# Context products of distances 3 and 4 made during attention and kept in DRAM, with every block folded

## Chip, core and metric

The kernel runs on one core of one Trainium2 chip. The metric is device time in microseconds (us) of one execution; where several runs are given, their median. The engines are called by the profile's names: PE is TensorE (PEld is its weight loads), DVE is VectorE, ACT is ScalarE, POOL is GpSimd, SP is SyncE, whose queue issues every DMA of this kernel.

## What is computed

The reference is a decoder layer with three residual stages, each followed by a layer norm. Shapes: x and the context are 16 x 256 x 512 (batch, sequence, width).

```
x = layernorm(x + attention(x, w_q, w_k, w_v, w_o))      # 16 heads of 32, causal, quantised projections
x = layernorm(x + xattn(ctx, ctx, x, ssm_kernel, D))     # below
x = layernorm(x + ffn(x, gamma, W))                      # RMS norm, 8-bit rounding, one product

# xattn: x and the context are read as 256 "channels" (32 heads of 8) of length 512
kv  = einsum('bhil,bhjl->bijhl', ctx, ctx)               # products of every pair of a head's 8 channels
y   = causal convolution of kv with ssm_kernel[h]  +  kv * D[h]
out = einsum('bijhl,bhil->bjhl', y, x)
```

In the second stage k and v are the same tensor, so the 8 x 8 products of a head are symmetric in i and j. They are stored by distance d = j - i modulo 8: distances 0 to 3 have 8 products each, distance 4 has 4, which makes 36 products by 16 batches = 576 columns (`NPAIR`).

## The kernel before

**First stage, attention.** Work goes by batch. `step(b)` (lines 538 to 598) is written out by hand in four groups g = 0 to 3, one for each set of four attention heads. The order of calls in it is the order of the instructions on every engine: in this part PE, ACT, DVE, POOL and SP each run their queue in program order, and an instruction that waits holds everything behind it on its engine. A group has `scan` of batch b+1 (PE scores, then row maxima on DVE, L341 and L346) and `weigh` of batch b (PE scores again, exponential on ACT L386 into a tile `p`, then on POOL two selects L390 and the sum `both` L396). `values` of a group (PE L409, L416) reads `p` and comes just ahead of the next group's `weigh`. In the last batch (`last_step`) the order differs: two `weigh` run before the first `values`.

The input of a later batch goes through: `fetch_x(b+3)` (DMA L233), scales on DVE, scaling on POOL (L182, in group 2), rounding on ACT (L188), and in group 3 `turn_in(b+3)`, two DMA transposes on SP (L279) into the tile `xit`. The first reader of `xit` is `project_qk` for that batch, called in group 0 of the next step (four PE matmuls, L293). `turn_out` (L473) is a like pair of transposes for the attention output in group 2.

The tiles `p` and `low` come from the pool `hp` with three buffers each.

**Second and third stage.** One loop over the 32 heads h (lines 1091 to 1126), again in a hand-written order. Head h needs the tile `kv` (its 576 columns for four blocks of 128 positions), made from the context `c` by ACT (squares, L760) and POOL (`multiply(k)` for k = 1, 2, 3; L754; `multiply(2)` also makes distance 4). `block(h, lb)` for lb = 0 to 3 makes the convolution on PE (`products`, L785: 2(lb+1) matmuls, which the trace lists as 4, 8, 12 and 16) into a PSUM tile `y` with two buffers, and `with_queries` (DVE, L797 to L812) multiplies by x into the tiles `own` (pool `op`, four buffers) and `turn`. `add` (POOL, L960) adds `turn` into `own`; for blocks in `FOLDED` a second instruction (L962) folds four parts into two. `read` (PE, L820) transposes and sums the parts of `own`: two transposes for a folded block, four for block 0, which isn't folded. PE's order in one turn of the loop is: block 0, read of block 2 of head h-1, block 1, read of block 3 of h-1, block 2, the feed-forward product of h-2 (L907), read of block 0 of h, block 3, read of block 1 of h. After these come norm and feed-forward on DVE and ACT.

The loads of head h+2 (`c` L745 and L746, `w` L749), one DMA transpose and one store of a result are on SP in each turn.

Of the kernel before, what the change touches and what calls it, by code (L numbers as in the profile page):

```python
# [9 lines left out]
F32 = mybir.dt.float32  # L10
BF16 = mybir.dt.bfloat16
AF = mybir.ActivationFunctionType
ALU = mybir.AluOpType
AX = mybir.AxisListType

P = 128
# [16 lines left out]
def decoder_kernel(ctx: ExitStack, tc: tile.TileContext, x, ctx_t, w_q, w_k, w_v, w_o, ker, d_skip, gamma, w_f, out):  # L33
# [6 lines left out]
    w_inv = const.tile([P, 5], F32, name="w_inv")  # L40
    q_scale = const.tile([P, 1], F32, name="q_scale")
    taps = taps_pool.tile([XH, E + P], F32, name="taps")

    kept = ctx.enter_context(tc.tile_pool(name="kept", bufs=1))
    x1t = kept.tile([P, XH, NB, XD, B], F32, name="x1t")
# [169 lines left out]
    att = ExitStack()  # L215
    qk = att.enter_context(tc.tile_pool(name="qk", bufs=3, side="right"))
    vp = att.enter_context(tc.tile_pool(name="vp", bufs=3, side="right"))
    hp = att.enter_context(tc.tile_pool(name="hp", bufs=3, side="right"))
    bp = att.enter_context(tc.tile_pool(name="bp", bufs=2, side="right"))
    ps_s = att.enter_context(tc.tile_pool(name="ps_s", bufs=1, space=PSUM, side="right"))  # L220
    NT = S // P
# [138 lines left out]
    def lay_turned(m, b):  # L360
        t = terms[b % 2]
        tp = ps.tile([P, S], BF16, name="tpn", tag="misc")
        for i in range(NT):
            nc.tensor.transpose(tp[:, i * P : (i + 1) * P], t[:, i, :], ident_h)
        m.low = hp.tile([P, S], BF16, name="low")
        nc.scalar.copy(m.low, tp)
# [156 lines left out]
    def keep(m, b, ts=(0, 1)):  # L523
        nh = P // XD
        for t in ts:
# [5 lines left out]
                tp.rearrange("p c (h i) -> p c h i", i=XD),  # L531
            )

    def on(stage, b, *more):
        if 0 <= b < B:
            stage(batches[b], *more)

    def step(b):


        on(scan, b + 1, 0)
        on(lay_turned, b, b)
        on(fetch_x, b + 3, b + 3)
        on(fetch_again, b - 1, b - 1)
        on(values, b - 1, NB - 1)
        on(begin_batch, b + 2)
        scale = project_qk(batches[b + 2], 0, (0,), wait=True) if b + 2 < B else None
        on(spread, b + 2, b + 2)
        on(save_sums, b - 1)
        on(moments, b - 2)  # L550
        if scale:
            scale()
        on(weigh, b, 0)
        if b < 2:
            weight_round(3 + b, 0)
        if b == 0:
            weight_size(4, nc.scalar)
        on(project_qk, b + 2, 1)
        on(normalize, b - 2)
        on(divide_sums, b - 1)  # L560
        on(divide, b - 1, 0)

        on(scan, b + 1, 1)
        on(divide, b - 1, 1)
        on(out_scales, b - 1)
        on(values, b, 0)
        on(weigh, b, 1)
        if b == 0:
            weight_scale(4, weight_total(ps, 4))
        if b < 2:  # L570
            weight_round(3 + b, 1)
            weight_store(3 + b, 0)
        on(project_qk, b + 2, 2)
        on(out_scaled, b - 1)
        on(keep, b - 2, b - 2)

        on(scan, b + 1, 2)
        on(fetch_scales, b + 3, b + 3)
        on(out_rounded, b - 1)
        on(turn_out, b - 1)  # L580
        on(project_v, b + 2, 0)
        on(values, b, 1)
        on(values_scale, b + 3)
        on(fetch_scaled, b + 3, b + 3)
        on(weigh, b, 2)
        on(project_v, b + 2, 1)
        on(project_qk, b + 2, 0, (1,))
        if b < 2:
            weight_store(3 + b, 1)

        on(scan, b + 1, 3)
        on(project_qk, b + 2, 3)
        on(lay, b + 1, b + 1)
        on(fetch_rounded, b + 3)
        on(turn_in, b + 3, b + 3)
        on(values, b, 2)
        on(weigh, b, 3)
        on(close, b - 1)

    def last_step():  # L600


        k, n, m = batches[B - 3 :]
        lay_turned(m, B - 1)
        moments(k)
        weigh(m, 0)
        fetch_again(n, B - 2)
        values(n, NB - 1)
        save_sums(n)
        weigh(m, 1)  # L610
        normalize(k)
        divide_sums(n)
        divide(n, 0)
        divide(n, 1)
        out_scales(n)
        weigh(m, 2)
        values(m, 0)
        out_scaled(n)
        weigh(m, 3)
        n.oi = [rounded(ap, "oq0", n.ots[0])]  # L620
        values(m, 1)
        n.oi.append(rounded(ap, "oq1", n.ots[1]))
        values(m, 2)
        n.oit = kp.tile([P, NT, NB, P], BF16, name="oit")
        for t in range(NT):
            transposed(ps, n.oit[:, t], n.oi[t])
        close(n)
        fetch_again(m, B - 1)
        keep(k, B - 3, (0,))
        values(m, 3)  # L630
        save_sums(m)
# [97 lines left out]
    with ExitStack() as l2:  # L729
# [2 lines left out]
        ps_y = l2.enter_context(tc.tile_pool(name="ps_y", bufs=2, space=PSUM, side="right"))  # L732
        pb = l2.enter_context(tc.tile_pool(name="pb", bufs=1, side="right"))
        gam = pb.tile([P, E], F32, name="gam")
        op = l2.enter_context(tc.tile_pool(name="op", bufs=4, side="right"))


        turns = [pb.tile([P, 4, P], F32, name=f"turn{i}") for i in range(NB)]
# [2 lines left out]
        def prepare(h):  # L741


            c = lp.tile([P, NB, EXT, B], F32, name="c")
            nc.sync.dma_start(c[:, :, 0:XD, :], ctx_t[h])  # L745
            nc.sync.dma_start(c[:, :, XD:EXT, :], ctx_t[h][:, :, 0 : EXT - XD, :])  # L746

            w = lp.tile([P, E], F32, name="w")
            nc.sync.dma_start(w, bass.AP(taps.tensor, taps.offset + h * (E + P), [[1, P], [1, E]]))  # L749

            kv = cp.tile([P, NB, NPAIR], F32, name="kv")

            def part(at, n, i, d):
                nc.gpsimd.tensor_tensor(  # L754
                    kv[:, :, at : at + n * B].rearrange("p c (i b) -> p c i b", b=B),
                    c[:, :, i : i + n, :], c[:, :, i + d : i + d + n, :], ALU.mult,
                )

            def square():
                nc.scalar.activation(  # L760
                    kv[:, :, 0:P].rearrange("p c (i b) -> p c i b", b=B), c[:, :, 0:XD, :], AF.Square
                )

            def multiply(k):
                part(k * P, XD, 0, k)
                if k == 2:
                    part(4 * P, 4, 0, 4)

            q = cp.tile([P, NB, EXT, B], F32, name="q")

            def copy(c=slice(0, NB)):
                nc.scalar.copy(q[:, c, 0:XD, :], x1t[:, h, c])
                nc.scalar.copy(q[:, c, XD:EXT, :], x1t[:, h, c, 0 : EXT - XD, :])

            return w, kv, q, multiply, copy, square

        FOLDED = (1, 2, 3)
        Y0 = E - HALF

        def products(lb, w, kv):  # L780
# [161 lines left out]
        def multiply(m, k):  # L942
            m.inputs[3](k)

        def copy(m, *blocks):
            m.inputs[4](*blocks)

# [14 lines left out]
                nc.gpsimd.tensor_tensor(own[:, 0:2, :], own[:, 0:2, :], own[:, 2:4, :], ALU.add)  # L962

        def read(m, lb):
            if lb == 0:

                m.tok = ps_k.tile([P, NB, P], F32, name="tok")
            total(lb, m.parts.pop(lb), m.tok)
# [11 lines left out]
        def roots_of(cols):  # L980
            roots = Roots()
            roots.quarter = sm.tile([P, 3], F32, name="quarter")
            roots.root = sm.tile([P, 3], F32, name="root")
            roots.cols = cols
            return roots

        def last_heads(three):

            early, prev, last = heads[XH - 3 :]
            one, end = roots_of(slice(0, 1)), roots_of(slice(0, 1))  # L990
            read(last, 2)
            read_all(last, 3)
            second_moments(last, three)
            engine_roots(three)
            second_centred(last)
            newton(three)
            second_max(last)
            inverse_roots(three)
            second_norm(last, three)
            finish(early, three, XH - 3)  # L1000
            feed_product(prev)
            feed_forward(prev, one)
            last.fit = fp.tile([P, NB, P], BF16, name="fit")
            transposed(ps2, last.fit, last.fi)
            engine_roots(one)
            newton(one)
            inverse_roots(one)
            finish(prev, one, XH - 2)
            feed_product(last)
            feed_forward(last, end)  # L1010
            engine_roots(end)
            newton(end)
            inverse_roots(end)
            finish(last, end, XH - 1, shared=True)
# [4 lines left out]
        first_head = heads[0]  # L1019
        with tc.manual_schedule(engines=by_hand):  # L1020
            load(first_head, 0)
            load(heads[1], 1)
            nc.sync.dma_start(gam, gamma.partition_broadcast(P))
            multiply(first_head, 1)
# [6 lines left out]
            for t in range(NT):  # L1031
# [2 lines left out]
                m.ots[t] = scaled(ap, f"oq{t}", m.o[:, t, :], m.mul_o[t])  # L1034
                if t == 0:
                    moments(n)
            multiply(first_head, 3)
            square(first_head)
            m.oit = kp.tile([P, NT, NB, P], BF16, name="oit")
            transposed(ps, m.oit[:, 0], rounded(ap, "oq0", m.ots[0]))  # L1040
# [30 lines left out]
            for h in range(XH):  # L1071
# [2 lines left out]
                on(load, h + 2, h + 2)  # L1074
                on(add, h - 1, 3)
                on(block, h, 0)
                on(read, h - 1, 2)
                on(multiply, h + 1, 1)
                on(square, h + 1)

                on(block, h, 1)
                on(add, h, 0)
                on(read, h - 1, 3)
# [11 lines left out]
                if h > 0:  # L1095
                    inverse_roots(roots)
                on(add, h, 1)
                on(read, h, 0)
                on(multiply, h + 1, 3)
                on(second_norm, h - 1, roots)  # L1100
                on(turn, h - 1)
                on(finish, h - 3, roots, h - 3)
# [44 lines left out]
```

## Time and profile before

| what | value |
|---|---|
| median of 3 runs | 865.26 us (864.24 to 866.11) |
| the profiled execution | 861.76 us, its span 860.0 us |
| mean granted TensorE clock | 0.988 |
| attention, one `step` | 25.1 us; PE busy 24.72, POOL 12.54 |
| second part, one head | 12.40 us; PE busy 12.26, DVE 10.87, POOL 11.53 |
| kernel's DMA traffic | 64.51 MB, mean 75 GB/s |

The profile shows one execution. A group line has: source line, engine, operation, tiles written <- read, shape, count, then busy time and mean duration. The timeline has start and duration in us, and in square brackets how long the engine sat idle ahead of the instruction and who released it. A line of the chain of waits has a start, a duration, and what the chain was in at that time. For a DMA on SP the duration is what the queue spends on issuing it; the landing is told apart. Line numbers are those of the kernel before.

### The profile page before, as it was taken

To read this page: it belongs to the slowest core of one execution; us is meant where nothing else is said; L and a number is where in the kernel's file an instruction comes from. 1 tells how busy PE (TensorE), PEld (TensorE's weight loads), DVE (VectorE), ACT (ScalarE), POOL (GpSimd) and SP (SyncE) were. 2 spreads that over 40 slices of the span, in tenths; PEclk is the share of its full clock that TensorE was granted. 3 is DMA by queue.
4 is the path that set the end of the run, shared out by engine and by line. 5 is a ranking of instruction groups with operands and counts; after the bars stand their busy time and mean duration, and the time that the engine had idled before them with its cause. 6 is when DMAs were issued, how large, how long until landed. Compare 5 with 4: busy or idle time off the path is not lost.

```text
span 860.0 us, 20228 instructions
## 1 busy us (share of the span) xinstructions
PE 803.8 (93%) x7754; PEld 555.9 (65%) x7754; DVE 690.5 (80%) x1889; ACT 427.0 (50%) x707; POOL 583.4 (68%) x652
## 2 busy tenths in 40 slices
PE   4889999999999999998878999999999999999993
PEld 3556666666666666665646767776777677777762
DVE  6757887788888778876666888988898889888885
ACT  6555655556565555655644334433443444344434
POOL 5265544545454454544639999999999999999980
PEclk9999999999999999999979999999999999999997
DMA  9111222333122222211320233223323332333211
GB/s 319 45 33 53 66 69 69 75 76 76 26 63 68 71 75 76 51 39 35 88 65 19 69 99 95 71 81 99 88 67 91 99 84 68 95 98 74 75 38 55
DMA packets 102207, 64.51 MB, mean 75 GB/s; under 512 B 66464, under 2 KB 83104, under 8 KB 102112
## 3 DMA queue, kind: packets, MB, share of 16 engines
q1 hardware_dynamic: 102112, 63.23, 27.5%
q8 instruction: 61, 1.00, 0.5%
q14 instruction: 34, 0.28, 0.1%
HBM read 43.34 MB, written 8.47 MB: 60 GB/s over the span
## 4 chain that ended last, share of the span: by engine, by line
PE 77%; DVE 10%; ACT 6%; issue 4%; POOL 2%; DMA 0%; ACTq 0%; DVEq 0%; POOLq 0%
PE y L785 32%; PE s L341 6%; PE acc L293 6%; PE s L381 5%; ACT p L386 4%; PE tok L820 4%; PE pv L409 4%; PE s L334 4%; PE acc_o L482 3%; DVE nmax L346 3%; PE acc_f L907 3%; PE sums L416 2%; PE s L374 2%; PE acc_v L311 2%; PE tp L528 1%
## 5 line engine op out<-in xcount | busy, mean ns | idle before, releaser
L785 PE MATMUL y<-kv,w 128*128 128x288 f32 x1280 | 335.0, 409 | 4.4 <-DVE turn L812 2.0
L785 PEld LDWEIGHTS y<-kv,w 128*128 128x128 f32 x1280 | 234.0, 191 | 64.9 <-PE tok L820 10.5
L960 POOL TENSOR_TENSOR own<-own,turn 128x512 f32<-128x512 f32 x127 | 161.7, 1274 | 21.1 <-DVE turn L812 11.0
L390 POOL TENSOR_SCALAR_AFFINE_SELECT p<-p 128x512 f32<-128x512 f32 x128 | 81.3, 659 | 139.5 <-ACT p L386 129.1
L754 POOL TENSOR_TENSOR kv<-c 128x512 f32<-128x512 f32 (+1 forms) x128 | 144.4, 1140 | 2.9 <-PE sums L416 2.9
L346 DVE TENSOR_REDUCE nmax<-s 128x4 f32<-128x512 f32 (+1 forms) x128 | 116.5, 952 | 35.5 <-PE s L341 35.5
L386 ACT ACTIVATE p<-s 128x1536 f32<-128x1536 f32 x64 | 92.9, 1452 | 70.3 <-PE s L381 70.2
L845 ACT ACTIVATE root<-quarter 128x3 f32<-128x3 f32 (+2 forms) x34 | 7.0, 204 | 159.5 <-DVE quarter L840 159.5
L396 POOL TENSOR_TENSOR both<-p 128x512 f32<-128x512 f32 x64 | 82.3, 1286 | 5.3
L797 DVE SCALAR_TENSOR_TENSOR own<-y,q 128x128 f32<-128x128 f32 x128 | 36.7, 286 | 50.5 <-PE y L785 42.6
L962 POOL TENSOR_TENSOR own<-own 128x256 f32<-128x256 f32 x95 | 69.1, 727 | 7.5
L293 PE MATMUL acc<-xit,w 128*128 128x256 bf16 x504 | 68.9, 276 | 3.6 <-DVE w L158 3.4
L800 DVE TENSOR_TENSOR own<-y,q 128x384 f32<-128x384 f32 x128 | 70.1, 548 | 0.0
L803 DVE TENSOR_TENSOR turn<-y,q 128x384 f32<-128x384 f32 x128 | 70.1, 548 | 0.0
L820 PEld LDWEIGHTS tok<-ident,own 128*128 128x128 f32 x318 | 37.7, 141 | 38.5 <-POOL own L962 26.0
L293 PEld LDWEIGHTS <-w 128*128 128x128 bf16 x512 | 45.9, 99 | 24.1 <-issue 8.5
L820 PE MATMUL tok<-ident,own 128*128 128x128 f32 x318 | 58.7, 283 | 2.4 <-issue 1.2
L341 PE MATMUL s<-kt,qt 32*128 32x128 f32 (+1 forms) x1024 | 60.0, 348 | 0.0
L381 PE MATMUL s<-qt,kt 32*128 32x256 f32 (+1 forms) x1024 | 57.4, 335 | 0.0
L409 PE MATMUL pv<-p,va 128*32 128x256 f32 (+1 forms) x1024 | 54.9, 332 | 0.0
L421 ACT COPY ot<-pv 128x256 f32<-128x256 f32 x64 | 23.9, 373 | 50.8 <-PE pv L409 50.2
L334 PE MATMUL s<-mask,ident_h 128*128 128x256 bf16 x256 | 38.3, 271 | 11.0 <-ACT p L386 9.9
(148 smaller groups left out, 1359.8 us busy)
## 6 DMA issues: line engine op xcount, KB each, us to landing
xt<-in_x SPq DMA_DIRECT2D x16, 512.0 KB, 4.1
xr<-in_x SPq DMA_DIRECT2D x16, 512.0 KB, 4.6
c<-in_ctx_t SPq DMA_DIRECT2D x32, 256.0 KB, 3.3
w<-taps SPq DMA_DIRECT2D x32, 256.0 KB, 4.1
out_y<-res SPq DMA_DIRECT2D x31, 256.0 KB, 2.3
c<-in_ctx_t SPq DMA_DIRECT2D x32, 128.0 KB, 3.2
x1t<-in_w_q SPq DMA_DIRECT2D x1, 1024.0 KB, 6.6
x1t<-in_w_k SPq DMA_DIRECT2D x1, 1024.0 KB, 9.4
```

What stands on the lines that cost most here:

```text
L293: nc.tensor.matmul(acc[:, j, :], w[:, c, o * P : (o + 1) * P], m.xit[:, c].rearrange("p t k -> p (t k)"), start=(c == 0), stop=(c == NB - 1),)
L341: nc.tensor.matmul(s[:, r, lo:hi], m.qt[rows, g, q0 : q0 + P], m.kt[rows, g, 0:nk], start=False, stop=True, skip_group_check=True,)
L346: nc.vector.tensor_reduce(m.nmax[:, t, :, g], s[:, :, cols], AX.X, ALU.max, negate=True)
L381: nc.tensor.matmul(s[:, r, lo:hi], m.kt[rows, g, k0 : k0 + P], m.qt[rows, g, q0:S], start=False, stop=True, skip_group_check=True,)
L386: nc.scalar.activation(p, s[:, :, 0 : 3 * P], AF.Exp)
L390: nc.gpsimd.affine_select(out=own, in_=own, compare_op=ALU.is_ge, fill=0.0, base=0, pattern=[[0, 4], [1, P]], channel_multiplier=-1,)
L396: nc.gpsimd.tensor_tensor(both, p[:, :, P : 2 * P], p[:, :, 2 * P : 3 * P], ALU.add)
L409: nc.tensor.matmul(acc[rows, q0:S], m.va[:, j, 4 * g + r, :], p[:, r, src], start=(j == 0), stop=(j == 1), skip_group_check=True, tile_pos ...
L754: nc.gpsimd.tensor_tensor(kv[:, :, at : at + n * B].rearrange("p c (i b) -> p c i b", b=B), c[:, :, i : i + n, :], c[:, :, i + d : i + d + ...
L785: nc.tensor.matmul(y[:, Y0 + k * HALF : Y0 + (k + 1) * HALF], lhs, kv[:, mb, k * HALF : (k + 1) * HALF], start=(mb == 0), stop=(mb == lb),)
L820: nc.tensor.matmul(tok[:, lb, :], lhsT=own[:, d, :], rhs=ident, is_transpose=True, start=(d == last), stop=(d == 0))
L960: nc.gpsimd.tensor_tensor(own[:, 0:4, :], own[:, 0:4, :], turns[lb], ALU.add)
```

## The change

1. A tile `far_d` in DRAM holds, for each of the 32 heads, the products of distances 3 and 4 (192 columns for each of four blocks, 384 KB a head).
2. From batch 2 on, attention makes these products: `far_load` (two DMAs) brings a head's context, `far_multiply` (two POOL instructions, 128x512 and 128x256) makes them, `far_store` (one DMA) writes them and issues the next head's load. POOL's part comes right after `weigh` of groups 0 and 2, and of group 3 in odd batches: 2 or 3 heads in a step, 32 in steps 2 to 14. The store and the next load are issued in the group after, just behind `scan`, and thus on SP ahead of what follows in that group. The tiles `far_c` and `far_kv` have one buffer each.
3. `hp` goes from three buffers to two.
4. In the head loop `multiply(3)` and the distance-4 part of `multiply(2)` are gone; `fetch_far` (one DMA a head) reads them from `far_d` into `kv`.
5. Block 0 is folded too (one more POOL instruction a head), its `read` has two transposes instead of four, and moves from ahead of block 3 to the next turn, behind block 0 of the next head. `op` goes from four buffers to five.

```diff
+    FAR = P + P // 2
+    far_d = taps_pool.tile([XH, P, NB, FAR], F32, name="far_d")
...
-    hp = att.enter_context(tc.tile_pool(name="hp", bufs=3, side="right"))
+    hp = att.enter_context(tc.tile_pool(name="hp", bufs=2, side="right"))
+    farp = att.enter_context(tc.tile_pool(name="farp", bufs=1, side="right"))
...
+    def far_load(h):
+        far.c = farp.tile([P, NB, SPAN, B], F32, name="far_c")
+        nc.sync.dma_start(far.c[:, :, 0:XD, :], ctx_t[h])
+        nc.sync.dma_start(far.c[:, :, XD:SPAN, :], ctx_t[h][:, :, 0 : SPAN - XD, :])
+
+    def far_multiply():
+        far.kv = farp.tile([P, NB, FAR], F32, name="far_kv")
+        for at, n, d in ((0, XD, 3), (P, 4, 4)):
+            nc.gpsimd.tensor_tensor(
+                far.kv[:, :, at : at + n * B].rearrange("p c (i b) -> p c i b", b=B),
+                far.c[:, :, 0:n, :], far.c[:, :, d : d + n, :], ALU.mult,
+            )
+
+    def far_store(h):
+        nc.sync.dma_start(far_d[h], far.kv)
+        if h + 1 < XH:
+            far_load(h + 1)
...
+    def far_step(b, g):
+        if b == 2 and g == 0:
+            far_load(0)
+        elif b >= 2 and far.stored < far.done:
+            far_store(far.stored)
+            far.stored += 1
+
+    def far_work(b, g):
+        if b >= 2 and far.done < XH and (g in (0, 2) or (g == 3 and b % 2)):
+            far_multiply()
+            far.done += 1
...
         on(scan, b + 1, 2)
+        far_step(b, 2)
...
         on(weigh, b, 2)
+        far_work(b, 2)
...
         on(scan, b + 1, 3)
+        far_step(b, 3)
         on(project_qk, b + 2, 3)
         on(lay, b + 1, b + 1)
         on(fetch_rounded, b + 3)
         on(turn_in, b + 3, b + 3)
         on(values, b, 2)
         on(weigh, b, 3)
+        far_work(b, 3)
...
-        op = l2.enter_context(tc.tile_pool(name="op", bufs=4, side="right"))
+        op = l2.enter_context(tc.tile_pool(name="op", bufs=5, side="right"))
...
             def multiply(k):
                 part(k * P, XD, 0, k)
-                if k == 2:
-                    part(4 * P, 4, 0, 4)
+
+            def fetch_far():
+                nc.sync.dma_start(kv[:, :, 3 * P : NPAIR], far_d[h])
...
-        FOLDED = (1, 2, 3)
+        FOLDED = (0, 1, 2, 3)
...
+            read(last, 0)
             read(last, 2)
             read_all(last, 3)
...
                 on(block, h, 0)
+                on(read, h - 1, 0)
                 on(read, h - 1, 2)
                 on(multiply, h + 1, 1)
                 on(square, h + 1)
 
+                on(fetch_far, h + 1)
                 on(block, h, 1)
                 on(add, h, 0)
                 on(read, h - 1, 3)
...
                 on(add, h, 1)
-                on(read, h, 0)
-                on(multiply, h + 1, 3)
```

The first head's own `multiply(3)`, in the passage between the two parts, is replaced by a `fetch_far` at its start. In groups 0 and 1 `far_step` and `far_work` stand at the like places.

More of the change, by code (lines that the diff above doesn't have):

```diff
@@ L532, in keep @@
             )
+    SPAN = XD + 3
+    class Far:
+        pass
+    far = Far()
+    def far_load(h):
[13 more added lines that the diff above has]
+            far_load(h + 1)
+    far.done = far.stored = 0
+    def far_step(b, g):
[8 more added lines that the diff above has]
+            far.done += 1
     def on(stage, b, *more):
@@ L541, in step @@
         on(scan, b + 1, 0)
+        far_step(b, 0)
         on(lay_turned, b, b)
@@ L553, in step @@
         on(weigh, b, 0)
+        far_work(b, 0)
         if b < 2:
@@ L563, in step @@
         on(scan, b + 1, 1)
+        far_step(b, 1)
         on(divide, b - 1, 1)
@@ L567, in step @@
         on(weigh, b, 1)
+        far_work(b, 1)
         if b == 0:
@@ L604, in last_step @@
         lay_turned(m, B - 1)
+        far_step(B - 1, 0)
         moments(k)
@@ L773, in copy @@
                 nc.scalar.copy(q[:, c, XD:EXT, :], x1t[:, h, c, 0 : EXT - XD, :])
-            return w, kv, q, multiply, copy, square
-        FOLDED = (1, 2, 3)
+            return w, kv, q, multiply, copy, square, fetch_far
+        FOLDED = (0, 1, 2, 3)
         Y0 = E - HALF
@@ L943, in multiply, with fetch_far @@
             m.inputs[3](k)
+        def fetch_far(m):
+            m.inputs[6]()
         def copy(m, *blocks):
@@ L964, in read @@
         def read(m, lb):
-            if lb == 0:
+            if not hasattr(m, "tok"):
                 m.tok = ps_k.tile([P, NB, P], F32, name="tok")
@@ L1021, in decoder_kernel @@
             load(first_head, 0)
+            fetch_far(first_head)
             load(heads[1], 1)
@@ L1036, in decoder_kernel @@
                     moments(n)
-            multiply(first_head, 3)
             square(first_head)
```

## The prediction

> **What bounds the kernel now.** I read the page's engine shares and its 40 slices first, then engine busy time in two long windows, the chain of waits through a head, and the timeline of one attention step. The windows (length, then busy time with instruction counts of PE, PEld, DVE, ACT, POOL; then clock, DMA share, GB/s) give:
>
> ```profile
> PE   4889999999999999998878999999999999999993
> POOL 5265544545454454544639999999999999999980
> 100.00:400.00 300.00, 294.23 (x4456) 197.64 (x4455) 243.66 (x473) 171.93 (x237) 148.82 (x189) 1.00 0.25 61
> 486.00:842.00 356.00, 351.81 (x1554) 251.85 (x1553) 312.13 (x1094) 149.47 (x315) 327.68 (x313) 1.00 0.30 81
> ```
>
> The reader is to see that PE is full in both parts (98% and 99%), while POOL is half empty in attention and 92% busy in the head loop. What counts is whose wait ends last. Through one head the chain stays on PE:
>
> ```profile
> 614.03 0.44 PE tok L820 x4
> 614.47 3.88 PE y L785 x16
> 618.35 0.22 PE tok L820 x2
> 618.57 0.97 PE y L785 x4
> 619.54 0.42 PE tok L820 x2
> 619.96 0.13 issue
> 620.09 2.18 PE y L785 x8
> ```
>
> PE ends block 3 (x16) at 618.35, but block 1 of the next head (x8) starts only at 620.09. It needs the `y` buffer that block 3 used, and DVE frees that one at 619.93 (timeline, last instruction of `with_queries`). DVE is thus a close second bound:
>
> ```profile
> 609.98 0.29 DVE L797 SCALAR_TENSOR_TENSOR own<-y,q 128x128 f32<-128x128 f32 x1 [1.04 <-PE y L785]
> ...
> 618.46 0.29 DVE L797 SCALAR_TENSOR_TENSOR own<-y,q 128x128 f32<-128x128 f32 x1 [0.22 <-PE y L785]
> ...
> 560.69 0.29 DVE L797 SCALAR_TENSOR_TENSOR own<-y,q 128x128 f32<-128x128 f32 x1 [1.39 <-PE tok L820]
> ...
> 568.87 0.29 DVE L797 SCALAR_TENSOR_TENSOR own<-y,q 128x128 f32<-128x128 f32 x1
> ```
>
> From block 1's L797 to block 3's is 8.48 us when DVE waits for PE, and 8.18 in the one head where it started late and waited for nothing. Attention, one step:
>
> ```profile
> 207.66 2.50 SPq L279 DMA_TRANSPOSE xit<-xq_i  x2
> 210.27 0.52 SPq L233 DMA_DIRECT2D xt<-in_x  x1
> ...
> 208.02 1.27 POOL L396 TENSOR_TENSOR both<-p 128x512 f32<-128x512 f32 x1
> 212.90 1.23 POOL L390 TENSOR_SCALAR_AFFINE_SELECT p<-p 128x512 f32<-128x512 f32 x2 [3.61 <-ACT p L386]
> ...
> 215.90 0.61 PE L293 MATMUL acc<-xit,w 128*128 128x256 bf16 x4
> ```
>
> The two transposes of the next batch are issued at 207.66, land by 211.4 (2.5 us after the second) and are read by PE at 215.90: 4.5 us to spare. POOL has a gap of 3.6 us between 209.29 and 212.90.
>
> **The change, part by part.** *Head loop, PE.* `read` of block 0 goes from four transposes to two; the 0.44 us between L907 and the 16 matmuls goes, and two transposes (0.22) come where PE now waits for DVE. So block 3 ends 0.44 earlier. What is late next is DVE: its 8.18 us from block 1 to block 3, then 3.92 (568.87 to 572.79) until block 1 of the next head. The loop becomes 8.18 + 3.92 = 12.10 instead of 12.40, a gain of 0.30 a head; not 0.44, since DVE takes the rest. PE alone would need less: 2.18 + 0.38 + 2.91 + 0.86 + 3.88 to the end of block 3, then 0.22 + 0.97 + 0.44 to block 1, 11.84. About 28 heads run in this steady state: 8.4 us. *Head loop, POOL.* Out go 1.28 (L754, 128x512) and 0.73 (128x256), in comes 0.73 (L962): 11.53 becomes 10.3, and POOL is never last. Only the first heads gain: at 449.1 to 453.3 the chain runs over POOL (L754 1.24, L960 1.25, then "issue" 1.18) to the `read` ahead of block 3, and PE is free from 452.1 while that block starts at 453.94. Of 1.8 I take 1.2, and 0.7 for the next two heads. Sum for the loop: -10.3, from -6 (0.2 a head, the idle time in brackets) to -14 (0.44 a head).
>
> *Head loop, DMA.* `fetch_far` (384 KB) is issued behind `w` at about 609.4. `w`, issued at 608.72, lands 4.4 us later, so the new one lands near 614.5; block 0 of the next head reads it at 618.4. Hidden; should that cover go, it costs what it is late in each head. In SP's order the DMA transpose L902 comes 8 us later, so nothing waits for it. The fifth `own` buffer covers the later `read`.
>
> *Attention, POOL.* 32 times 1.96 us (the L754 pair at 612.17) comes into 13 steps. The gaps behind `both` are 3.61 (group 2), 3.52 (group 0) and 2.21 (group 3), so each is covered: 0. In odd batches group 3's context lands at about 216 instead of 215.49, which eats its 0.25 of slack; at worst 0.5 in six steps, 3 us.
>
> *Attention, SP: the added wait.* In group 3 the store of group 2's products is ahead of `turn_in`. It waits for POOL, and behind it on SP stand the two loads, both transposes, then `xt` and `xr`. Step by step: `both` of group 2 ends at 209.29, the products at 211.25, SP sees it within 0.1 at 211.33. Issuing a store takes 0.62 to the next (as L927 to L745), the loads 0.62 and 0.74 (L745, L746), so the first transpose starts at 213.31 instead of 207.66, the second 1.25 later, landing 2.45 after that: 217.0. PE wants it at 215.90. The 4.5 us of slack become a stall of 1.1 us, and PE has nothing else in its order. It comes back every step because `both` moves with PE; it concerns steps 2 to 12 (`turn_in` ends with batch 15), 11 stalls. The transposes also share the queue with 736 KB just issued; `xt` and `xr`, 1024 KB, took 5.0 us from issue to landing, so some overlap is left. Ends: 0.5 (if each of the three DMAs took only the 0.41 of `xr`) and 2.5 (if the loads land at their slowest, 4.6 us, and the transposes' data all come behind). I take 1.4, near the unloaded sum: 11 x 1.4 = +15.4, from +5.5 to +27.5.
>
> The trace has `c` landing 3.2 us after issue (4.6 at most), here at 215.8, ahead of the transposes. [...]
>
> The other transposes (L473, 202.49) come behind a store that waits for group 0's products (198.7 in this step's time) and end their queue at 200.8: no loss. `xt` is late by 5 to 10 us, against a use 18 us after its issue: no loss.
>
> *Last step, two `p` buffers.* In steady state a group's `values` is ahead of the next `weigh`, so two suffice: 0. In `last_step` the exponential of group 2 (420.62) now waits for `values` of group 0 (421.2, +0.6), and that of group 3 (423.32) for `values` of group 1 (about 424.9, +1.6). Behind it on ACT is the rounding L188 (424.67), which is on the chain: +1.6, from 0 to +2.2.
>
> Sum: -10.3 + 15.4 + 1.6 = +6.7 against the profiled 861.76 us (span 860.0 and 1.8 around it), which lies 3.5 under the median of the runs shown. Put on the median: 865.26 + 6.7 = **872.0**.
>
> **Rivals.** (1) *Faster: SP is held for less.* The place is the store ahead of `turn_in`; the gain of 8.7 that is left without stalls is lost at 0.79 us a stall. For it: that is only 0.3 under my unloaded sum, and issue times of 0.41 exist. Against: three DMAs plus the 4.0 us POOL delay are all rows of this trace. With 0.3 a stall: 860; with none: 856.6. (2) *The loop keeps its time*: DVE's 8.18 was seen in one head only; if a head gains 0.1, the loop gives -5 and the time is 877 to 878. (3) *Transfers collide*: 2.5 us a stall gives 884. For it: 736 KB right ahead in the one queue; against: the data should be through at about 215.2. (4) *It doesn't do what it says*: the instruction order shows 64 more POOL multiplies in attention and 128 more DMAs, so no.
>
> **How the numbers follow.** Measurement can tell about 0.2%, 1.7 us. Forecast (stall of 1.0 to 2.0, 867 to 879): 0.60. Within 0.2% (stall near 0.8): 0.08. Rival 1: 0.17. Rival 2: 0.09. Rival 3: 0.06. Slower 0.60 + 0.09 + 0.06 = 0.75. Range 861 to 884: it takes in part of rival 1 and nearly all above.
>
> **What would show it.** In the profile after: L279's successor issued about 4.0 us after `both` of group 2 ends, PE's xit matmul with idle time put down to a DMA, the attention step at 26.5 instead of 25.1 for 11 steps; a head at 12.10 with no idle time ahead of block 3's L797; ACT's exponential waiting for PE in the last step. A step still at 25.1 proves the stall wrong; a head at 12.40 proves the DVE reading wrong; 11.84 would mean that PE alone sets it.

## The result and the profile after

The changed kernel takes 877.31 us (median of 4 runs, 875.94 to 880.7) against 865.08 us (median of 4, 864.24 to 866.11) of the kernel before in the same job: ratio 1.0147, 95% interval 1.0115 to 1.0178. It is slower. The profiled execution took 875.94 us with a span of 874.2, 14.2 more than the 860.0 of before.

The page's slices of PE and POOL for the changed kernel, and its busy time in a window of attention and one of the head loop (columns as before; line numbers from here on are those of the kernel that ran):

```profile
PE   4889999999888999999778999999999999999994
POOL 5265657666575675766663988898888888888880
100.00:400.00 300.00, 275.84 (x4100) 186.44 (x4136) 237.38 (x444) 162.22 (x225) 191.95 (x233) 0.99 0.50 127
500.00:850.00 350.00, 341.00 (x1476) 250.66 (x1503) 311.37 (x1098) 149.57 (x315) 298.29 (x290) 1.00 0.44 117
```

The reader is to see eights among the nines of PE in the first half: in attention PE fell from 98% to 92% busy, while POOL rose from 50% to 64%. In the loop PE goes from 99% to 97% and POOL from 92% to 85%. So the loss is in attention and isn't POOL's load. The marks below are DVE instructions, one in each attention step (the row maximum of the divided output) and one in each block (L849); times in us.

| stretch | before | after | difference |
|---|---|---|---|
| 11 attention steps | 276.0 | 297.6 | +21.6 |
| last full step to the first block of the loop | 26.1 | 29.8 | +3.7 |
| head loop, first block to last | 395.9 | 385.6 | -10.3 |

In the loop (timeline of DVE's L849 in one head; block 1 at 606.03, block 3 at 614.21, block 1 of the next head at 618.13) nothing is waited for ahead of block 3, and the head takes 12.10:

```profile
606.03 0.29 DVE L849 SCALAR_TENSOR_TENSOR own<-y,q 128x128 f32<-128x128 f32 x1 [1.05 <-PE y L837]
...
614.21 0.29 DVE L849 SCALAR_TENSOR_TENSOR own<-y,q 128x128 f32<-128x128 f32 x1
...
618.13 0.29 DVE L849 SCALAR_TENSOR_TENSOR own<-y,q 128x128 f32<-128x128 f32 x1 [1.04 <-PE y L837]
```

Attention now has a wait that before had none of. The waits view (waiting <- awaited: us in all, how often, longest) and the timeline of one of the milder steps:

```profile
PE acc L296 <- DMA xit<-xq_i: 13.5, 8, 2.7
ACT p L389 <- PE sums L419: 3.1, 2, 2.0
```

```profile
327.64 1.97 POOL L552 TENSOR_TENSOR far_kv<-far_c 128x512 f32<-128x512 f32 x2
...
329.63 0.37 SPq L558 DMA_DIRECT2D far_d<-far_kv  x1
...
330.11 0.57 SPq L546 DMA_DIRECT2D far_c<-in_ctx_t  x1
...
331.48 2.56 SPq L282 DMA_TRANSPOSE xit<-xq_i  x2
...
335.39 0.60 PE L296 MATMUL acc<-xit,w 128*128 128x256 bf16 x4 [1.00 <-DMA xit<-xq_i]
```

SP waits for POOL's products until 329.61, spends 1.85 us on the store and two loads, and only then starts the transposes, 3.80 us after `both` ended at 327.68; PE waits 1.00 for them. But the steps aren't alike. They took 26.72, 26.57, 26.52, **29.26, 27.38, 27.54, 28.89**, 26.11, 26.19, 26.26 and 26.19 us, against 25.09. The first of the four in bold:

```profile
192.28 2.58 SPq L282 DMA_TRANSPOSE xit<-xq_i  x2
...
197.92 1.01 PE L296 MATMUL acc<-xit,w 128*128 128x256 bf16 x4 [2.71 <-DMA xit<-xq_i]
...
199.37 1.59 PE L384 MATMUL s<-qt,kt 32*128 32x256 f32 x13
```

Here PE starts 5.64 us after the issue, not 3.91, and the same four matmuls take 1.01 us instead of 0.60: the granted clock is 0.5 from 197.9 to 201.3. So two things are to be explained that the forecast did not have: why the transposes land late in four steps, and what the slow clock costs.

### The profile page after: what moved, and what is told of

It is laid out like the page before. It is cut to its first block, busy times and chain, and to the rows that moved or that the text cites. A ratio compares the mean times of both kernels' runs of the same rounds, so it can differ in the third digit from the quotient of the medians.

```text
span 874.2 us, 20247 instructions
## 1 busy us (share of the span) xinstructions
PE 792.6 (91%) x7614; PEld 555.6 (64%) x7690; DVE 697.2 (80%) x1889; ACT 426.9 (49%) x707; POOL 605.9 (69%) x684
## 4 chain that ended last, share of the span: by engine, by line
PE 67%; DVE 10%; ACT 10%; issue 5%; POOL 4%; DMA 3%; ACTq 0%; POOLq 0%; DVEq 0%
PE y L837 29%; PE acc L296 6%; PE s L344 6%; PE s L384 5%; ACT p L389 4%; DVE nmax L349 4%; PE s L337 3%; PE acc_o L485 3%; DMA xit<-xq_i 3%; PE acc_f L959 3%; PE pv L412 3%; ACT res L978 2%; PE s L377 2%; ACT q L824 2%; PE acc_v L314 2%
## 5 line engine op out<-in xcount | busy, mean ns | idle before, releaser
L1017 POOL TENSOR_TENSOR own<-own 128x256 f32<-128x256 f32 x127 | 92.2, 726 | 9.9
L805 POOL TENSOR_TENSOR kv<-c 128x512 f32<-128x512 f32 x64 | 81.4, 1272 | 4.7 <-PE sums L419 4.7
L849 DVE SCALAR_TENSOR_TENSOR own<-y,q 128x128 f32<-128x128 f32 x128 | 36.7, 286 | 42.3 <-PE y L837 33.7
L552 POOL TENSOR_TENSOR far_kv<-far_c 128x512 f32<-128x512 f32 x64 | 62.8, 1002 | 6.6 <-DMA far_c<-in_ctx_t 6.2
L302 DVE SCALAR_TENSOR_TENSOR qt<-acc,q_scale,inv_row 128x256 f32<-128x256 f32 (+1 forms) x45 | 26.2, 582 | 31.2 <-PE acc L296 18.5
```

Of the source, the lines that this page charges most:

```text
L805: nc.gpsimd.tensor_tensor(kv[:, :, at : at + n * B].rearrange("p c (i b) -> p c i b", b=B), c[:, :, i : i + n, :], c[:, :, i + d : i + d + ...
```

## The experiments

Theory at the start: the far store and loads ahead of `turn_in` in group 3 cost the steps, by SP's wait and by their issue; the loop's gain is as forecast; the two `p` buffers cost the last step. Later a further point came in: a 16 KB packet of the instruction queue delays transposes that are in flight. Each ratio is against runs of the kernel before in the same job.

**1. The store and loads behind the transposes.**

```diff
         on(scan, b + 1, 3)
-        far_step(b, 3)
...
         on(turn_in, b + 3, b + 3)
+        far_step(b, 3)
         on(values, b, 2)
```

> The changed kernel with one call moved: in group 3 the store of the far products stands behind turn_in on SP instead of ahead of it. Same work, same traffic. Theory (the queue is held): the transposes of xit start again right after the rounding, some 4 us earlier, PE's wait for xit goes from every step and the attention step is 25.1 us again; 21.6 us of attention time and the half-clock windows that follow such waits go, so 877.3 - 21.6 = 855.7, 853 to 858. Rival (GpSimd's added work or the added traffic slows attention wherever the store stands): the step stays above 25.7 and the time above 863.

Measured: 855.62 us (854.71 to 858.1), ratio 0.9907, 0.9883 to 0.9931. Ten of the eleven steps take 25.13 or 25.14, and one 26.25, in which PE waited for DVE's row maxima. The order on SP, from the timeline:

```profile
209.06 2.50 SPq L282 DMA_TRANSPOSE xit<-xq_i  x2
...
210.62 1.97 POOL L552 TENSOR_TENSOR far_kv<-far_c 128x512 f32<-128x512 f32 x2
...
212.62 0.36 SPq L558 DMA_DIRECT2D far_d<-far_kv  x1
```

The transposes are out before the products are begun, and PE waits for them nowhere. All of the work and all of the transfers are still there, so in ten of the eleven steps neither POOL's 64 multiplies nor the traffic costs attention more than 0.04 us (and experiment 5 has the same 25.13 with the two `p` buffers alone): the place of one call costs it. What held DVE up in the one step stays open. Moved, the change is faster than before.

**2. Only the loads behind.** The store with its wait stays ahead of `turn_in`, the two loads go behind it.

```diff
-            far_store(far.stored)
+            far_store(far.stored, g != 3)      # False: without the next load
...
         on(turn_in, b + 3, b + 3)
+        far_late()                             # the load
         on(values, b, 2)
```

> The changed kernel with the store still ahead of turn_in in group 3, but the two loads behind it. Theory (the wait is the sum of POOL's products and the issue times): the loads' 0.62 + 0.74 us leave the path, the unloaded stall of 1.0 to 1.3 us becomes 0 to 0.2, and only steps in which the transposes land late (by 1 to 1.7 us) still stall; attention gives back 14 to 21 of its 21.6 us: 856 to 864, middle 860. Rival (a transpose behind a waiting store is late whatever stands between): the stall stays above 0.8 in every step and the time above 870.

Measured: 872.5 us (870.14 to 876.45), ratio 1.0113, 1.0074 to 1.0153. The reason held and the time did not. In five of the eleven steps the transposes now land 0.4 to 0.5 us before PE reads them: the wait and the store's issue, without the 1.3 us of load issues, just fit into the old slack. In the other six PE starts within 0.14 us of the landing, after 0.25 to 1.51 us of idle time, 5.1 in all (the profile puts two of these down to the DMA and four to DVE instructions that ended just before); in all six a 16 KB packet of the instruction queue (experiment 4) begins between 0.5 us ahead of the issue and the landing. And ten steps take 25.4 to 27.7, for a wait of another kind as well (waits view, then timeline):

```profile
POOL far_kv L552 <- DMA far_c<-in_ctx_t: 25.2, 11, 3.5
```

```profile
358.06 1.97 POOL L552 TENSOR_TENSOR far_kv<-far_c 128x512 f32<-128x512 f32 x2 [2.56 <-DMA far_c<-in_ctx_t]
...
363.30 0.43 PE L419 MATMUL sums<-both,col 128*32 128x128 f32 x8 [0.71 <-POOL both L399]
```

The context lands later, POOL stands still ahead of its multiply with `both` of the next group queued behind it, and PE waits for `both` (six times in the steps, 3.7 us). The tile `far_c` has one buffer, so a load can be neither early nor late. I had counted only the wait that was to go.

**3. Traffic ahead, but no wait.** Experiment 1, with three DRAM to DRAM copies (0.6 MB, nothing reads the results) ahead of the transposes.

```diff
         if 2 <= b < B - 3:
+            nc.sync.dma_start(idle_d[b, 0], ctx_t[b])
+            nc.sync.dma_start(idle_d[b, 1], ctx_t[b + 1])
+            nc.sync.dma_start(idle_d[b, 2, :, :, 0:3, :], ctx_t[b][:, :, 0:3, :])
         on(turn_in, b + 3, b + 3)
```

> The experiment with the store behind the transposes (855.6 us), and ahead of the two transposes of each step three copies from DRAM to DRAM of about the size of the changed kernel's store and loads (0.6 MB), which wait for nothing and whose results nothing reads. My theory (a stall needs the wait for POOL and the three issues together, 2.5 + 1.9 us against about 4.5 us of slack): no stall, steps near 25.1 us and 855 to 857.5 us. Rival (what delays the transposes is the transfers right ahead of them): PE waits for the transposes by 0.7 us or more in most steps, 863 us and above.

Measured: 857.22 us (855.44 to 858.15), ratio 0.9925, 0.9898 to 0.9952. PE waits for no transposes, and all steps but one (27.23, where PE waited for DVE's row maxima) take 25.13 or 25.14. The test is of the traffic: the copies are issued mostly before the transposes' input is ready, so these start at most 0.9 us later against PE's read than in experiment 1. Behind the copies their last byte comes 3.27 to 3.78 us after the issue in the six steps without a packet of the instruction queue (3.25 to 3.27 in experiment 1), so traffic right ahead costs them 0.5 us at most. Three issues that stand between POOL's products and the transposes, with nothing to wait for, were not run alone; that 1.85 us would fit into 4.5 us is arithmetic. With experiment 2 the account is that the wait just fits, and that with the two loads' issues on top the sum goes over the slack.

**4. Moving the instruction packets.** What set the four late steps apart? The trace has the packets of each DMA queue. The queue of kind "instruction" that follows PE's pace moved 61 packets of 16 KB, about one per 250 PE instructions (the page's line has queue, kind, packets, MB and share of the 16 DMA engines):

```profile
q8 instruction: 61, 1.00, 0.5%
```

In each of the four late steps one of them fell 1.6 to 2.7 us behind the issue of the transposes, in the other seven none came between issue and landing. That is a coincidence until the packets are moved. So the changed kernel was run with small matmuls at the very start, 64 or 96 of them, which nothing reads.

```diff
         constants()
+        idle = ps.tile([P, S], F32, name="idle", tag="misc")
+        for i in range(64):                    # 96 in the second
+            nc.tensor.matmul(idle[:, 0:8], ident_h, ident_h[:, 0:8], start=True, stop=True)
         fetch_x(m, 0)
```

> The changed kernel with 64 small matmuls (128 PE instructions with their weight loads) at the very start, ahead of all other PE work, whose result nothing reads; attention itself is the same. In the changed kernel PE waited over 2 us for the transposes in the steps that followed their issue at 192, 222, 249 and 276 us, and in each of these a 16 KB packet of the instruction queue fell 1.6 to 2.7 us behind the issue; such a packet came about every 256 PE instructions. My theory (the packet delays the transposes): 128 instructions more move the packets by half their distance, some 4.3 us, so these four steps fall to waits of about 1.0 us, and other steps (those where the packet now falls 0.6 to 3 us behind the issue) get waits over 1.5 us. Rival (the four steps are late for a reason of their own, a place in DRAM or the transfers of those heads): the same four steps keep waits over 2 us. The total time is no test, since the matmuls may lengthen the start.

> As the experiment with 64 small matmuls, with 96 of them (192 PE instructions). My theory: counted from the nearer packet the packets come 64 instructions, some 2.1 us, later: behind the landing in the four late steps, more than 3.5 us from the issue in the later ones. So the four steps fall to waits of about 1.0 us and at most one or two others get over 1.5; the two stretches of half clock in attention go with the late steps; the span from the first to the last full attention step shrinks by 4 to 8 us and the time is 870 to 875 us, with up to 3 us more if the matmuls lengthen the start. Rival (reasons of their own): the same four steps keep waits over 2 us, 877 us or more.

> The kernel with 64 small matmuls ahead once more, now timed. Where a packet falls is set by the place in the program, so my theory expects the same steps again: eight near 26.2 us, none with a wait over 2 us, and 867.5 to 870.5 us, 7 to 10 us under the changed kernel (877.3) with nothing taken out of it. Rival (the one look was a lucky execution): 873 us or more in most runs.

The wait of PE ahead of its first read of `xit` in the eleven steps, with the place of the nearest packet against the issue of the transposes (us; the last byte is that of the transposes' own packets; in steps 1 to 3 of the changed kernel and step 11 with 64 matmuls the profile names a DVE instruction as what came last):

| step | changed kernel: packet, last byte, wait | 64 matmuls ahead | 96 matmuls ahead |
|---|---|---|---|
| 1 | -2.3, 3.32, 1.52 | -5.3, 3.32, 1.04 | **2.1, 4.27, 2.15** |
| 2 | -2.1, 3.33, 1.39 | -4.5, 3.34, 0.98 | **1.8, 4.51, 2.33** |
| 3 | -2.1, 3.33, 1.33 | -4.8, 3.32, 1.02 | **2.4, 4.73, 2.58** |
| 4 | **2.7, 4.90, 2.71** | -4.0, 3.37, 1.05 | 4.9, 3.33, 1.03 |
| 5 | **2.1, 4.37, 2.18** | -3.1, 3.31, 1.00 | **2.4, 4.81, 2.68** |
| 6 | **1.6, 4.51, 2.36** | -3.0, 3.32, 1.00 | -4.7, 3.35, 1.04 |
| 7 | **2.4, 4.35, 2.24** | -2.6, 3.33, 1.02 | -4.6, 3.35, 1.05 |
| 8 | 4.0, 3.35, 0.91 | -2.1, 3.34, 1.05 | -4.1, 3.31, 0.91 |
| 9 | 7.3, 3.33, 1.00 | -2.3, 3.32, 1.61 | -3.1, 3.35, 1.05 |
| 10 | 5.5, 3.34, 1.08 | -2.5, 3.32, 1.86 | -3.1, 3.36, 1.06 |
| 11 | -4.6, 3.32, 1.00 | -2.1, 3.32, 1.32 | -2.7, 3.37, 1.03 |

Step 3 and step 4 with 96 matmuls ahead:

```profile
171.41 2.56 SPq L282 DMA_TRANSPOSE xit<-xq_i  x2
...
176.90 1.01 PE L296 MATMUL acc<-xit,w 128*128 128x256 bf16 x4 [2.58 <-DMA xit<-xq_i]
...
200.53 2.56 SPq L282 DMA_TRANSPOSE xit<-xq_i  x2
...
204.47 0.60 PE L296 MATMUL acc<-xit,w 128*128 128x256 bf16 x4 [1.03 <-DMA xit<-xq_i]
```

The late steps go where the packets go, and all eight bold cells have a packet 1.6 to 2.7 us behind the issue. The rival (the same four steps stay late) is out: with 64 matmuls ahead no wait reaches 2 us, and with 96 three of the four fall to 1.0. What I said of the places was only half right: with 96 I expected one or two others over 1.5 us, and there were four late steps; with 64 the waits of 1.61 and 1.86 have a packet 2.3 and 2.5 us *ahead* of the issue. There the transposes aren't slow (3.32) but are issued late: a load that SP issues in 0.57 us elsewhere takes 1.22, with a packet in flight beside it (321.84 to 322.85).

```profile
322.16 1.22 SPq L546 DMA_DIRECT2D far_c<-in_ctx_t  x1
...
328.05 0.60 PE L296 MATMUL acc<-xit,w 128*128 128x256 bf16 x4 [1.61 <-DMA xit<-xq_i]
```

Steps 1 to 3 of the changed kernel are of that kind too (that load took 1.06, 1.00 and 0.86 us). Times: 868.89 us in the first run with 64 matmuls, and 872.05 (868.57 to 872.72) in five more, ratio 1.008, 1.0053 to 1.0106; 874.58 (872.55 to 877.16) with 96, ratio 1.0113, 1.0096 to 1.013. The 867.5 to 870.5 that I expected of the former missed the median. In the profile of these five the last three steps were 26.91, 28.29 and 28.30, with two stretches of half clock, though no wait reached 2 us. The median with 96 lies in the 870 to 875 that I expected, but not for my reason: in its profile, that of its slowest run, the eleven steps did not shrink by 4 to 8 us (299.7 against 297.6). Even so, some 4 to 5 us of the changed kernel's time go with where the packets fall (12.2 us over the kernel before of the same job as it stands, 8.4 with 64 matmuls ahead; ratios 1.0147 and 1.008).

**5. Two `p` buffers in the kernel before.**

```diff
-    hp = att.enter_context(tc.tile_pool(name="hp", bufs=3, side="right"))
+    hp = att.enter_context(tc.tile_pool(name="hp", bufs=2, side="right"))
```

> The kernel before with the pool of p and low cut from three buffers to two, nothing else. Theory: only the last step of attention is longer, by the waits of two exponentials for the values of two groups before, 1.6 to 2.2 us: 865.1 + 2 = 867, 866.3 to 867.8. Rival (the whole 3.7 us by which the last step grew is the buffers'): 868.8. Rival (nothing): 865.

Measured: 867.06 us (865.76 to 870.45), ratio 1.0044, 1.0028 to 1.0059. In the last step ACT has the same two waits as in the changed kernel, 1.13 and 2.00 us. The stretch to the loop takes 29.8 instead of 26.1; 3.4 us of half clock (431.0 to 434.4) are in it that the kernel before doesn't have, so the +3.7 is the waits, about 2, and the clock.

**6. A third `p` from the far tiles' memory.** Experiment 1, with `far_c` and `far_kv` laid into one tile of 6 KB per partition; in the last step, when the products are done, group 2's exponential writes there.

```diff
-        weigh(m, 2)
+        weigh(m, 2, far.all.rearrange("p (r k) -> p r k", r=4))
         values(m, 0)
```

> The experiment with the store behind the transposes (855.6 us), and in the last step the exponential of group 2 writes into the memory of the far products, which is free by then, so that three buffers serve the four groups as in the kernel before. My theory: the two waits of ACT in the last step (1.1 and 2.0 us) go, the step is 2.0 us shorter: 853.6 us, from 852.5 to 855. Rival (the last step is bound elsewhere, by the division of the batch before or by PE): 855 us and above.

Measured: 853.75 us (852.13 to 854.26), ratio 0.9886, 0.9864 to 0.9908: 1.9 us under experiment 1, and the best version here. The exponentials of groups 2 and 3 no longer wait for `values` (timeline):

```profile
424.90 1.44 ACT L390 ACTIVATE far<-s 128x1536 f32<-128x1536 f32 x1
...
427.59 1.45 ACT L390 ACTIVATE p<-s 128x1536 f32<-128x1536 f32 x1 [0.99 <-PE s L384]
```

**7. The loop's parts, one by one.** The fold alone in the kernel before, with the products still in the loop:

```diff
-        FOLDED = (1, 2, 3)
+        FOLDED = (0, 1, 2, 3)
...
                 on(block, h, 0)
+                on(read, h - 1, 0)
...
-                on(read, h, 0)
                 on(multiply, h + 1, 3)
```

> The kernel before with the head loop's half of the change alone: block 0 folded, its two transposes in the next turn, five own buffers; all products still made in the loop. Theory (POOL would become the bound): POOL's 11.53 us a head grow by 0.73 to 12.26, and with its handovers a head takes 12.25 to 12.4 instead of 12.10: at most 4 us less than before, 861 to 866. Rival (the fold alone brings the gain and the far products are not needed): a head at 12.10 and 855.

Then, on experiment 1, the products alone (`FOLDED = (1, 2, 3)`, block 0's read in its old place), and the fold with the read kept in its old place:

> The experiment with the store behind the transposes (855.6 us), but block 0 is not folded and its read keeps its old place with four transposes: only the far products are taken out of the head loop. My theory (PE and DVE set the head, POOL does not): a head falls back to 12.40 us and the time to 855.6 + 28 x 0.30 = 864.0 us, from 862.5 to 865.5, though POOL has 2 us less to do in each head. Rival (POOL's load was part of the 12.40): a head at 12.2 or less, 858 or less.

> The same experiment (855.6 us), block 0 folded, but its read (now two transposes) stays ahead of block 3 of its own head instead of moving a head on. My theory: block 3 ends 0.22 us later on PE than with the move, of which DVE's slack of 0.14 us (0.44 less 0.30) takes part, so a head is 12.18 us and the time 855.6 + 28 x 0.08 = 857.8 us, from 856.5 to 859.5. Rival: the fold makes the parts of block 0 ready later on POOL than PE wants them, PE waits ahead of block 3, and a head is 12.4 or more: 863 us and above.

| what is done | a head, us | loop, us | time, us | ratio and interval |
|---|---|---|---|---|
| nothing (before) | 12.40 | 395.9 | | |
| fold and move alone | 12.53 | 401.1 | 867.99 | 1.005, 1.0032 to 1.0067 |
| products alone | 12.40 | 395.8 | 865.73 | 1.0032, 1.0014 to 1.0049 |
| products and fold, read in place | 12.18 | 390.8 | 860.94 | 0.9972, 0.9955 to 0.9989 |
| all three (experiment 1) | 12.09 | 385.3 | 855.62 | 0.9907, 0.9883 to 0.9931 |

The groups of the fold alone, 500 to 850 us, show why it loses: the first line is POOL's `add`, the second PE's `read`.

```profile
L960 POOL TENSOR_TENSOR own<-own,turn 128x512 f32<-128x512 f32 x111 | 141.5, 1275 | 1.9 <-DVE res L863 1.8
...
L820 PE MATMUL tok<-ident,own 128*128 128x128 f32 x222 | 43.6, 279 | 23.5 <-POOL own L962 23.5
```

In the kernel before, POOL sat idle 19.6 us ahead of those `add`s. Here 1.9 are left: POOL has become the bound, and PE waits for it, 23.5 us in 28 heads. I had expected 861 to 866 us of the fold alone; it costs 5 us in the loop. The products alone take 2 us of POOL's work out of each head and gain nothing (the time is 0.2 above what I allowed), since PE and DVE set it. Only together do they pay. The read's place was forecast well in the steady state (12.18), but the time missed by 3.1 us: the first head alone takes 14.97 us there against 12.01, which I had not counted. PE waits there 1.18 us for POOL's fold of block 0, as the rival had it but in this head alone, and block 3's sixteen matmuls behind the wait take 5.73 us instead of the 4.05 of experiment 1, with half clock from 461.6 to 465.0.

## Why the prediction was right or wrong

The forecast was +6.7 us, 872.0, with a range of 861 to 884; measured are +12.2 and 877.31. The direction was right, and the time lies in the range; two of the three terms of the sum were too small.

*Head loop, PE and DVE (-10.3): right.* 8.18 and 3.92 are found as the prediction put them, 385.6 is 10.3 under 395.9; the last 28 of the 31 intervals between heads give 7.9 of it (8.4 forecast) and the first three 2.1 (1.9 forecast). Its reading that DVE takes the rest of the 0.44 held. That POOL "is never last" held for the whole change, and not for the fold by itself.

*Head loop, DMA, and attention, POOL (0 and 0): right.* PE waits for `far_d` nowhere, and experiment 1 does all 64 multiplies in attention at 25.13 a step.

*Attention, SP (+15.4): the mechanism was right, the size was off; +21.6.* SP's wait, three issues and two transposes are as told: 3.8 us from the end of `both` to the first transpose in the milder step, 4.0 forecast. The unloaded sum of 1.1 a stall was right as it stood: the steps without a packet in the way cost 1.0 to 1.2. I raised it to 1.4 for "some overlap" with the transfers, which the runs don't show: in steps 8 to 11 of the changed kernel, with 736 KB issued right ahead, the last byte came 3.32 to 3.35 us behind the issue, against 3.26 in the kernel before. Nor did the loads come last: both landed 0.9 to 2.7 us before the transposes in all eleven steps. What did raise it to 1.96 on average are the packets of the instruction queue: 0.3 to 0.5 us more in steps 1 to 3, and over a microsecond in the four late ones, two of which had half clock behind the wait (in step 4 the same matmuls 1.01 instead of 0.60; some 1.5 us a step). In the kernel before such packets fell on transposes as well (four of eleven, last byte up to 4.31 us behind the issue against 3.26), and the 4.5 us of slack paid for them. The step that failed is thus the assumption that a slack once used up costs only what the sum exceeds it by.

*Last step (+1.6): +3.7.* The waits measured 1.14 and 2.00, and experiment 6 gives 1.9 for both. The rest goes with a stretch of half clock, 450.5 to 453.9, that the prediction did not have: in experiment 1, with the same two waits and no half clock there, the whole stretch takes 27.5 us, +1.5 (28.1 in experiments 2 and 3). So the term was about right for the waits, and the clock's part was not in it.

*The rivals.* The price of the first, 856.6 without stalls, is met by experiment 1 with 855.6: it was the right account of what the change would be worth with the store elsewhere. Loops that keep their time (the second) are out with a head of 12.10. Transfers that collide (the third) are out by the 3.32 to 3.35 us above and by experiment 3; 2 us and more in a stall did come, but with the packets.

Not settled: why PE gets half the clock after some of these waits and not after others.

## What to carry to other kernels

SP issued in program order here, and the store that waited for POOL held back all that stood behind it: the first transpose came 3.80 us after the end of `both`, and with the store behind the transposes PE waited for them nowhere (25.13 or 25.14 in ten of the eleven steps). So put the store of a product behind the transfers that the next step needs, above all where the place costs nothing. Work taken off an engine that wasn't the bound paid only with something else that moved onto it: the products alone left the loop at 395.8 us against 395.9, the fold alone took 401.1, and both with the moved read 385.3. So cost such parts together and each alone. And slack that a profile shows may be in use: here the 4.5 us ahead of PE's first read covered delays (a last byte up to 4.31 us behind the issue against 3.26) that became visible only when the slack was gone.

## What the runs showed of the hardware

Transfers were late where a packet of the instruction queue fell on them. In the ten traces that had been taken before the packets were moved, 110 pairs of transposes: the last byte came 3.26 us (median of 68, at most 3.78) behind the issue where no packet fell between 1 us ahead of the issue and that byte, and 4.00 (median of 42, at most 4.90) where one did. The packets are of 16 KB each and follow PE's pace: 33 for 8236 PE instructions between 100 and 400 us of the changed kernel, one for 250, and 61 for the 15508 of the kernel before, one for 254. Their places go with the place in the program: the first eight, up to where the two kernels part, start at the same times within 0.3 us in the traces of both (24.7 and 24.8 the first, 95.2 and 95.4 the eighth). PE itself waited for no DMA in the eleven steps of the kernel before (the waits view has 2.5 us for ACT and nothing else), so there only the transfers show a delay.

Half clock came in stretches of 3.4, 6.8 or 10.2 us in attention and the passage behind it (3.4 from 197.9 and 10.2 from 460.8 in the changed kernel, 6.8 from 146.3 with 96 matmuls ahead), and began in or up to 1.7 us behind five of the eight bold waits of 2.15 to 2.71 us in the table (with 64 matmuls ahead also by waits of 1.68 to 1.86). No experiment here varied the idle time, so what length of wait brings half clock was not shown.
